# Projecting the selected keys and values of two sequences at once, and pricing TensorE's changes of mode in the planner

## The chip, the cores and the metric

The kernel runs on one NeuronCore of a Trainium2 chip, as one program. TensorE (PE) does the matmuls, VectorE (DVE), ScalarE (ACT) and GpSimd (POOL) the elementwise work, and SyncE (SP) issues all DMAs from one queue. The metric is the device time of one launch in microseconds (us), as the median of several runs; before the change it is 1702.44 us (three runs, 1701.02 to 1708.38).

## The reference

One post-norm decoder layer on x of shape (8, 256, 256) in f32: eight sequences of 256 tokens with 256 features. Three blocks follow each other, each with a residual and a layernorm:

```python
x = _layernorm(x + attn(x))          # three attentions, mixed by a gate
x = _layernorm(x + cross_attn(x, ctx))
x = _layernorm(x + moe_ffn(x))       # 8 experts of 256 -> 1024 -> 256, all evaluated
```

The first block holds three attentions of 16 heads with the same queries: over latent keys (causal), over the 64 selected tokens, and over windowed keys (causal). This change touches the second of them:

```python
scores = (x @ w_imp)[..., 0]
_, idx = jax.lax.top_k(scores, KEEP)             # KEEP = 64, per sequence
sel = jnp.take_along_axis(x, idx[:, :, None], axis=1)
ks = (sel @ w_selk)    # 64 x (16 heads x 96)
vs = (sel @ w_selv)    # 64 x (16 heads x 32)
```

The weights w_selk and w_selv are the same for all sequences.

## The kernel before

All of the work is written as Python generators ("threads") that yield operations, and a planner (`Machine`, L119) puts them in order when the program is built. For each operation it holds a guessed duration, and it keeps the time at which each engine is free, at which each buffer was written and used last, and the state of every pool of buffers. In each step (`run`, L213) it takes from each engine's candidates the one that can start first, or among those that can start within 0.1 us of it the one of lowest rank, and commits the earliest of these. The hardware then executes each engine's list strictly in that order, with semaphores for the dependencies; the guessed times only make the order. DMAs go the same way into the one list of SP: a DMA that waits for its buffer holds up all DMAs planned after it.

A thread's rank starts low for early sequences and grows by `AHEAD` = 4 for each sequence (`each`, L812). Attention work ranks by sequence; the experts (L1378) have rank 99, so they fill what attention leaves free on TensorE. The experts of a sequence can start only when both attention blocks of that sequence are done.

Per sequence s and group g of four heads (NHG = 4 groups): `project` (L827) makes queries, windowed keys and selected keys and turns them (rope); `first` (L958) makes the scores; `weighing` the softmax; `products` (L1048) the weighted values. Matmuls in which the contraction or the output has 32 rows run as groups of four in row or column bands of the array (names `s`, `sx`, `pkn`, `pvl` in row bands, `o`, `ox` in column bands; `mm(..., share=4)`); all others use the whole array. `group` (L288) joins matmuls into one planner operation and adds a fixed `extra` to its guessed time: 0.1 us for scores, 0.3 us for products.

Selection (`selection`, L654) works per sequence: scores to one row, eight rounds of top-8 on DVE, positions by a scan, transposed back with two small matmuls (`ppos`), a one-hot matrix on POOL, and the selected rows of x by matmul (`psel`). The result is copied twice over into `selT` (L688 to L704), so that the value projection (`pvs`, L709) yields the 64 selected values once on partitions 0 to 63 and once on 64 to 127; these are copied into the two diagonal blocks of `vs` (L378), of which there is one, so it is filled when the last products of the sequence before have been issued (L707). The selected keys are projected in `project` for each sequence and group: six matmuls of 128x128 weights with 64 columns (`pks`, L871 to L879). `lead(s)` (L724) returns s, so `two_` is never true.

Each f32 matmul of the program appears as two instructions in the profile.

Buffers that matter here: three tiles each for the expert weights W1 and W2 (`load_w`, L513, 512 KB per half expert, also used for staging the attention weights at the start in `rearrange`, L466), and three each for a sequence's x (`xT` transposed and `xr`, L494), which live from the load until the sequence's experts are done.

Of the kernel before, what the change touches and what calls it, by code (L numbers as in the profile page):

```python
# [17 lines left out]
P = 128  # L18
B, T, C = 8, 256, 256
H = 16  # L20
# [12 lines left out]
NEG = -1e30  # L33
LOWEST = -3.4028234663852886e38
QSCALE = 1.0 / math.sqrt(DH)
AHEAD = 4
ENGINES = {
    mybir.EngineType.PE,
# [17 lines left out]
class Op:  # L56
# [4 lines left out]
    def __init__(self, engine, us, outs, ins, issue, lag=0.0, size=0):  # L61
        self.engine, self.us, self.issue, self.lag, self.size = engine, us, issue, lag, size
        self.writes = [k for x in outs for k in Op.blocks(x)]
        self.reads = [k for x in ins for k in Op.blocks(x)]

    @staticmethod
    def blocks(ap):
# [51 lines left out]
class Machine:  # L119
    def __init__(self):  # L120
        self.free = dict.fromkeys(("PE", "DVE", "ACT", "POOL", "SP"), 0.0)
        self.written, self.used, self.touched = {}, {}, {}
        self.slots, self.tag, self.pending, self.given = {}, {}, {}, {}
        self.transfers = 0.0
        self.reserved = {}
        self.urgent = None
        self.threads = []
# [39 lines left out]

    def start(self, op):
        t = self.free[op.engine]
        for name, b in op.reads:  # L170
            if (name, b) not in self.written:
                return math.inf
            eng, at = self.written[name, b]
            t = max(t, at + (0.0 if eng == op.engine else 0.15))
            if b == PSUM and (name, b) in self.used:
                eng, at = self.used[name, b]
                t = max(t, at + (0.0 if eng == op.engine else 0.1))
        for name, b in op.writes:
            if name in self.pending:
                slots = self.slots[self.pending[name]]  # L180
                if len(slots) <= self.reserved.get(self.pending[name], 0):
                    return math.inf
                t = max(t, min(slots) + 0.1)
            else:
                t = max(t, self.given.get(name, -1.0) + 0.1)
            eng, at = self.used.get((name, b), ("", 0.0))
            t = max(t, at + (0.0 if eng == op.engine else 0.1))
            eng, at = self.written.get((name, b), ("", 0.0))
            if not (op.size and eng == op.engine):
                t = max(t, at + (0.0 if eng == op.engine else 0.15))  # L190
        return t

    def commit(self, op, t):
        for name, _ in op.writes:
            if name in self.pending:
                self.take(name)
        op.issue()
        end = self.free[op.engine] = t + op.us
        if op.size:
            self.transfers = max(self.transfers, end) + op.size / 330e3  # L200
            end = self.transfers + 2.5
        end += op.lag
        for k in op.reads:
            self.used[k] = (op.engine, max(end, self.used.get(k, ("", 0.0))[1]))
            self.touched[k[0]] = max(end, self.touched.get(k[0], 0.0))
        for k in op.writes:
            self.written[k] = (op.engine, end)
            self.touched[k[0]] = max(end, self.touched.get(k[0], 0.0))
# [50 lines left out]
def decoder_layer(ctx: ExitStack, tc: tile.TileContext, a: dict, out: bass.AP):  # L259
# [25 lines left out]
        n = in_.shape[0]  # L285
        return Op("PE", 0.11, [out], [in_], lambda: nc.tensor.transpose(out, in_, ident[:n, :n]), lag=0.17)

    def group(ops, extra=0.0):  # L288
        op = Op("PE", sum(o.us for o in ops) + extra, [], [], lambda: [o.issue() for o in ops], lag=0.17)
        op.writes = list(dict.fromkeys(k for o in ops for k in o.writes))  # L290
        op.reads = list(dict.fromkeys(k for o in ops for k in o.reads))
        return op

    def copied(dst, src):

        return V.tensor_copy(dst, src), A.copy(dst, src)
# [22 lines left out]
    def seen(*key):  # L319
        return lambda: (key if len(key) > 1 else key[0]) in done  # L320
# [145 lines left out]
    def rearrange(g):  # L466

        todo = (
            (wq, a["w_up"][0:QL], QL, 1, lambda o, i: V.tensor_scalar(o, i, QSCALE, None, ALU.mult)),
            (wkw, a["w_wink"], P, 2, A.copy),  # L470
            (wks, a["w_selk"], P, 2, G.tensor_copy),
        )
        staged = []
        yield seen("staged", g - 1) if g else seen("inputs")
        if g:
            yield seen("setup")
        for w, src, rows, k, _ in todo:
            t = three([P, 2, HG * DH], ("w1", "w2")[g % 2], "stage")
            staged.append(t)
            yield dma(t[0:rows, 0:k], src[:, bass.ts(g, HG * DH)].rearrange("(k p) c -> p k c", p=rows))  # L480
        done.add(("staged", g))
        for t, (w, src, rows, k, copy) in zip(staged, todo):
            for i in range(k):
                yield copy(
                    w[0:rows, i, g].rearrange("p i (h r) -> p i h r", h=HG),
                    t[0:rows, i].rearrange("p (h i r) -> p i h r", i=3, r=32),
                )
            m.release(t)
        done.add(("parts", g))
# [2 lines left out]
    xTs, xrs, cTs, w1s, w2s = {}, {}, {}, {}, {}  # L492

    def load_sequence(s):  # L494
        xTs[s] = t = three([P, 2, T], "xT", "xT")
        yield dma(t, kp(a["xT"][:, bass.ts(s, T)]))
        xrs[s] = t = three([P, 2, C], "xr", "xr")
        yield dma(t, a["x"][bass.ts(s, T), :].rearrange("(t p) c -> p t c", p=P))
        done.add(("x", s))

# [12 lines left out]
    def load_w(kept, tag, shape, source):  # L513

        yield seen("parts", NHG - 1)
        for n in range(B * E * 2):
            t = three(shape, tag, tag)
            yield dma(t, source(n // 2 % E, n % 2))
            kept[n] = t

# [133 lines left out]
    def selection(s, d):  # L654
# [36 lines left out]
        else:  # L691
            yield lambda: "selT" in pro[s - 1]
            both = pro[s - 1]["selT"]
        selT = both[:, :, 2 * n : 2 * n + 2]
        pg = mtile([P, 2, KEEP], "psel")
        yield group(
            [
# [3 lines left out]
            ]  # L701
        )
        m.release(hot)
        yield V.tensor_copy(selT, pg.unsqueeze(2).to_broadcast([P, 2, 2, KEEP]))  # L704
        m.release(pg)
        done.add(("selected", s))
        if s:  # L707
            yield seen("products", s - 1, NHG - 1)
        pv = mtile([P, H * VH], "pvs")  # L709
        yield group(  # L710
            [mm(pv, selT[:, k].rearrange("p i s -> p (i s)"), wvs[:, k, :], k == 0, k == 1) for k in range(2)]
        )
        used(lead(s))
        for i in range(2):
            yield copied(vs[bass.ts(i, KEEP), i], pv[bass.ts(i, KEEP)])
        m.release(pv)
        done.add(("selected values", s))

    def used(s):
        pro[s]["users"] -= 1  # L720
# [2 lines left out]

    def lead(s):  # L724

        return s

    def raw(s, d):

# [97 lines left out]
    def project():  # L827
        for s in range(B):
            yield 2 + AHEAD * s
            d = pro.setdefault(s, {})  # L830
            for g in range(NHG):
# [30 lines left out]

                ks = None
                if lead(s) == s:
                    two_ = False
                    yield seen("selected", s)
                    if two_:
                        yield seen("selected", s + 1)
                        stash = kept[g] = four([P, 3, KEEP], "stash", "stash")
                        yield m.claim(stash)  # L870
                    ks = mtile([P, 3, 1 + two_, KEEP], "pks")  # L871
                    sel = d["selT"][:, :, 1 : 3 if two_ else 2].rearrange("p k i s -> p k (i s)")
                    yield group(
                        [
                            mm(ks[:, i].rearrange("p n s -> p (n s)"), wks[:, k, g, i], sel[:, k], k == 0, k == 1)
                            for i in range(3)
                            for k in range(2)
                        ]
                    )  # L879
                    if g == NHG - 1:  # L880
                        used(s)
                    if two_:
                        yield copied(stash, ks[:, :, 1])
                    own = ks[:, :, 0]
                else:
                    own = kept[g]
# [21 lines left out]
    def latent_pairs(name):  # L908

        for s in range(B):  # L910
            yield 2 + AHEAD * s
            d = pro.setdefault(s, {})
            for g in range(2):
# [13 lines left out]
                        ops += [(p_[:, bass.ts(i, P)], lk[rows, bass.ts(i, P)], wkv[rows, g, 1]) for i in range(2)]  # L927
                if name != "kn":
                    ops = ops[0::2] + ops[1::2]
                yield group([mm(*op, share=2) for op in ops], 0.1)  # L930
                for n, p_ in enumerate(ps):
                    yield copied(t[:, n], p_)
                m.release(*ps)
# [6 lines left out]
    def scores(h, d, g, st, which):  # L940
# [4 lines left out]
        for qt, (lo, n) in enumerate(spans):  # L945
            for i in range(3):
                for j in range(HG):
# [5 lines left out]
                    ops.append(  # L953
                        mm(st[j][:, lo : lo + n], h["q"][rows, i, bass.ts(qt, P)], key, i == 0, i == 2, share=4)
                    )
        return group(ops, 0.1)

    def first():  # L958
        for s in range(B):
# [88 lines left out]
    def products():  # L1048
        for s in range(B):
            yield 3 + AHEAD * s  # L1050
            oT = None
            for g in range(NHG):
# [22 lines left out]
                def times(*blocks):  # L1075
                    ops = []
                    for n, (lo, hi, v, src, c) in enumerate(blocks):
                        for j in reversed(range(HG)):
# [7 lines left out]
                                    share=4,  # L1086
                                )
                            )
                    return group(ops, 0.3)

                yield times(
                    (0, T, lambda j: h["vw"][:, 0, bass.ts(j, VH)], pa, 0),
# [39 lines left out]
    def kept_in_dram(shape, name):  # L1132
        d = dram.tile(shape, F32, tag=name, name=name)
        Op.kept.add(d.tensor.name)
        return d
# [67 lines left out]
    def second():  # L1203
        for s in range(B):
# [23 lines left out]
            for g in range(NHG):  # L1228
                pr = three([P, HG * 2 * T], "p", "prx")
                yield m.claim(pr)  # L1230
                if g:
# [6 lines left out]
                        for qt in range(2)  # L1238
                        for j in range(4)
                    ],  # L1240
                    0.1,
                )
                d[g] = {"pr": pr, "st": st}
                done.add(("prx", s, g))
# [32 lines left out]
    def x_products():  # L1277
        for s in range(B):
            yield 3 + AHEAD * s
            for g in range(0, NHG, 2):  # L1280
# [8 lines left out]
                for n in range(2):  # L1289
# [13 lines left out]
                            for c in range(2)  # L1303
                            for j in reversed(range(4))
                        ],
                        0.3,
                    )
                    m.release(xt)
                yield copied(oT[:, g // 2, :], o)
# [143 lines left out]
    each(3, latents)  # L1453
    each(5, selection)
    each(7, gates)
    m.thread(5, context())
    m.thread(5, fetch())
    m.thread(99, experts())
# [96 lines left out]
```

## Time and profile before

| what | value |
|---|---|
| median of three runs | 1702.44 us |
| profiled execution | 1705.71 us, of which the span of instructions 1703.9 us |
| PE busy / weight loads (PEld) busy | 1632.8 us (96%) / 1344.4 us (79%) |
| DVE / ACT / POOL busy | 1178.6 / 573.7 / 601.1 us |
| DMA traffic | 326.82 MB, mean 192 GB/s |
| mean granted TensorE clock | 0.980 |
| expert matmuls `ph` and `py` | 2048 instructions each, 483.2 and 470.9 us |
| `pks` and `pvs` | 384 and 32 instructions, 48.0 and 16.5 us |

The busy time of a group is the union of its instructions' spans; matmuls are pipelined, so one of 256 columns spans some 380 ns while such matmuls start 216 ns apart. What a matmul costs the engine is therefore read from the distance of starts in the timeline, not from its own span. The expert matmuls start at 261.8 us; from 1584 us to the end only the experts of the last sequence are left.

### The profile page before, as it was taken

Reading aid. Unit: us, or ns where it says so; the run is one execution under the profiler, and the core shown is the slowest. Engines: PE = TensorE matmul, PEld = TensorE weight load, DVE = VectorE, ACT = ScalarE, POOL = GpSimd, SP = SyncE. Lnnn points to the kernel's source line nnn. Section 1 sums busy time; section 2 is a strip of 40 time slices with the busy share of each in tenths; the row PEclk is TensorE's granted clock in tenths of the full one; section 3 lists DMA queues with packets and bytes.
Section 4 is the critical chain, followed back from the end, with each engine's and each line's share of the span. In section 5 each row is a group of like instructions: output and inputs, shape, how many; then the busy total and the mean of one; then the engine's idle time right before and its main releaser. Section 6 shows DMA issues by size and latency. Waiting matters only on the chain.

```text
span 1703.9 us, 32142 instructions
## 1 busy us (share of the span) xinstructions
PE 1632.8 (96%) x12196; PEld 1344.4 (79%) x12196; DVE 1178.6 (69%) x2602; ACT 573.7 (34%) x2084; POOL 601.1 (35%) x799
## 2 busy tenths in 40 slices
PE   6999789999999999999999999998999999999998
PEld 4787567887788888887888788886888878888887
DVE  5988777777677856677866786677867777454333
ACT  2554453244324243254324343143422443021000
POOL 3766633444225332263323432343332542021000
PEclk8999898999999999999999999999999999999999
DMA  7212314567926686268563767447592687667452
GB/s 251 81 46 92 135 58 171 176 222 263 319 81 237 211 280 211 84 219 292 199 237 119 268 208 239 175 151 277 193 315 63 231 285 252 199 215 259 130 150 79
DMA packets 183785, 326.82 MB, mean 192 GB/s; under 512 B 12864, under 2 KB 105168, under 8 KB 176464
## 3 DMA queue, kind: packets, MB, share of 16 engines
q1 hardware_dynamic: 183632, 324.78, 56.4%
q8 instruction: 97, 1.59, 0.4%
q14 instruction: 56, 0.46, 0.1%
HBM read 235.60 MB, written 89.14 MB: 191 GB/s over the span
## 4 chain that ended last, share of the span: by engine, by line
PE 79%; issue 8%; DVE 7%; DMA 4%; ACT 1%; POOL 1%; SPq 0%; POOLq 0%; DVEq 0%; ACTq 0%
PE ph L280 22%; PE py L280 22%; PE s L280 8%; PE o L280 4%; PE pk L280 3%; PE pyo L280 3%; PE pks L280 2%; PE pv L280 2%; DMA xpt<-prx 2%; PE sx L280 2%; PE pq L280 2%; PE ox L280 2%; DMA prx<-prx 2%; PE pkm L280 1%; DVE pr L98 1%
## 5 line engine op out<-in xcount | busy, mean ns | idle before, releaser
L280 PE MATMUL ph<-xT,w 128*128 128x256 f32 x2048 | 483.2, 386 | 1.4 <-DVE pl L98 0.6
L280 PE MATMUL py<-w,h 128*128 128x256 f32 x2048 | 470.9, 382 | 0.0
L280 PEld LDWEIGHTS ph<-xT,w 128*128 128x128 f32 x2048 | 387.8, 193 | 68.2 <-issue 10.2
L280 PEld LDWEIGHTS py<-w,h 128*128 128x128 f32 x2048 | 385.3, 191 | 60.0 <-issue 7.9
L98 DVE TENSOR_SCALAR h<-ph,b 128x256 f32<-128x256 f32 x323 | 153.9, 481 | 122.1 <-PE ph L280 119.4
L98 ACT ACTIVATE h<-ph,b 128x256 f32<-128x256 f32 x189 | 89.4, 473 | 323.6 <-PE ph L280 316.6
L98 POOL TENSOR_TENSOR prx<-prx,sumsx 128x512 f32<-128x512 f32 x128 | 129.8, 1045 | 150.9 <-DVE sumsx L98 99.8
L98 DVE SCALAR_TENSOR_TENSOR xr<-py,rw,xr 128x256 f32<-128x256 f32 x128 | 61.0, 478 | 152.5 <-PE py L280 152.2
L98 ACT ACTIVATE prx<-sx,nmx 128x256 f32<-128x256 f32 x256 | 117.1, 486 | 67.9 <-DVE nmx L98 47.8
L98 POOL TENSOR_TENSOR kx<-turn 128x64 f32<-128x64 f32 (+1 forms) x128 | 67.0, 541 | 203.3 <-DVE turn L98 195.6
L98 POOL TENSOR_TENSOR pr<-pr,wpr 128x256 f32<-128x256 f32 (+2 forms) x128 | 129.6, 1043 | 0.0
L98 ACT ACTIVATE pl<-pl,nmpl 128x128 f32<-128x128 f32 (+1 forms) x256 | 113.2, 446 | 13.8 <-DVE nmpl L98 11.8
L98 ACT ACTIVATE pr<-pr,nmpr 128x128 f32<-128x128 f32 (+1 forms) x256 | 113.1, 447 | 0.0
L98 DVE TENSOR_TENSOR pr<-s,causal 128x256 f32<-128x256 f32 x128 | 74.2, 580 | 42.7 <-PE s L280 28.3
L98 POOL TENSOR_TENSOR rstd<-var,nhalf 128x2 f32<-128x2 f32 x24 | 17.2, 718 | 230.4 <-DVE var L98 229.8
L280 PE MATMUL s<-kx,q 32*128 32x320 f32 (+1 forms) x1536 | 95.5, 383 | 2.0 <-ACT prx L98 1.9
L98 POOL TENSOR_TENSOR q<-turn 128x256 f32<-128x256 f32 x64 | 45.6, 729 | 138.4 <-DVE turn L98 136.8
L98 POOL TENSOR_TENSOR pl<-pl,wpl 128x512 f32<-128x512 f32 x64 | 92.5, 1466 | 2.7
L98 DVE TENSOR_REDUCE nmx<-sx 128x2 f32<-128x512 f32 x128 | 79.2, 681 | 11.4 <-PE sx L280 11.4
L280 PEld LDWEIGHTS s<-kx,q 32*128 32x128 f32 x1536 | 70.9, 185 | 19.6 <-issue 7.0
L98 DVE TENSOR_TENSOR pl<-s,causal 128x256 f32<-128x256 f32 x128 | 74.5, 582 | 12.0 <-PE s L280 5.8
L98 DVE TENSOR_REDUCE nmpr<-pr 128x4 f32<-128x256 f32 (+2 forms) x128 | 80.3, 672 | 0.0
(213 smaller groups left out, 2437.0 us busy)
## 6 DMA issues: line engine op xcount, KB each, us to landing
w<-in_W SPq DMA_DIRECT2D x256, 512.0 KB
pr<-pr SPq DMA_DIRECT2D x28, 1024.0 KB
pa<-pr SPq DMA_DIRECT2D x28, 1024.0 KB
prx<-prx SPq DMA_DIRECT2D x28, 1024.0 KB
xpt<-prx SPq DMA_DIRECT2D x28, 1024.0 KB
pl<-pl SPq DMA_DIRECT2D x28, 768.0 KB
pb<-pl SPq DMA_DIRECT2D x28, 768.0 KB
xT<-in_xT SPq DMA_DIRECT2D x8, 256.0 KB
```

The source lines that it names most:

```text
L98: return Op(self.name, us, outs, ins, lambda: getattr(self.engine, kind)(*args, **kw))
L280: lambda: nc.tensor.matmul(out, lhsT, rhs, start=start, stop=stop, skip_group_check=share > 1),
```

## The change

Sequences 2 and 3, 4 and 5, and 6 and 7 form pairs; 0 and 1 stay alone. For a pair, the selected rows of both stand side by side in `selT`. The keys are projected for both at once in the first sequence's `project` (128 columns in place of 64); the second's share is copied to a `stash` tile in SBUF. The values are projected for both at once (64 rows each of one output), copied to SBUF, written to DRAM, and read back into the two blocks of `vs` by two DMAs per sequence, in a thread of its own; the sequences that stay alone go the same way. The planner now knows for each TensorE operation whether it is tiled, and adds 0.3 us to the start of a full one after a tiled one and 0.09 us the other way round; the fixed extras shrink. The pools change: W1 and W2 from three tiles to two each, x from three to four; the staging at the start alternates between the W1 and W2 tiles.

```diff
+LEAVE, ENTER = 0.3, 0.09
...
     def start(self, op):
         t = self.free[op.engine]
+        if op.engine == "PE" and self.tiled != op.tiled:
+            t += LEAVE if self.tiled else ENTER
...
         end = self.free[op.engine] = t + op.us
+        if op.engine == "PE":
+            self.tiled = op.tiled
...
-            t = three([P, 2, HG * DH], ("w1", "w2")[g % 2], "stage")
+            t = two([P, 2, HG * DH], ("w1", "w2")[(g + len(staged)) % 2], "stage")
...
-        xTs[s] = t = three([P, 2, T], "xT", "xT")
+        xTs[s] = t = four([P, 2, T], "xT", "xT")
...
-        xrs[s] = t = three([P, 2, C], "xr", "xr")
+        xrs[s] = t = four([P, 2, C], "xr", "xr")
...
-            t = three(shape, tag, tag)
+            t = two(shape, tag, tag)
...
-        yield V.tensor_copy(selT, pg.unsqueeze(2).to_broadcast([P, 2, 2, KEEP]))
+        yield V.tensor_copy(both[:, :, n], pg)
         m.release(pg)
         done.add(("selected", s))
-        if s:
-            yield seen("products", s - 1, NHG - 1)
+        if lead(s + 1) == s:
+            return
+        rows = (n + 1) * KEEP
         pv = mtile([P, H * VH], "pvs")
         yield group(
-            [mm(pv, selT[:, k].rearrange("p i s -> p (i s)"), wvs[:, k, :], k == 0, k == 1) for k in range(2)]
+            [
+                mm(pv[0:rows], both[:, k, 0 : n + 1].rearrange("p n s -> p (n s)"), wvs[:, k, :], k == 0, k == 1)
+                for k in range(2)
+            ]
         )
         used(lead(s))
-        for i in range(2):
-            yield copied(vs[bass.ts(i, KEEP), i], pv[bass.ts(i, KEEP)])
+        sv = one([P, H * VH], "sv", "sv")
+        yield copied(sv[0:rows], pv[0:rows])
         m.release(pv)
-        done.add(("selected values", s))
+        pro[lead(s)]["sv"] = dv = kept_in_dram([P, H * VH], f"sv{lead(s)}")
+        yield dma(dv[0:rows], sv[0:rows])
+        m.release(sv)
+        done.add(("selected values kept", lead(s)))
+
+    def selected_values():
+        for s in range(B):
+            yield 5 + AHEAD * s
+            yield seen("selected values kept", lead(s))
+            if s:
+                yield seen("products", s - 1, NHG - 1)
+            for i in range(2):
+                yield dma(vs[bass.ts(i, KEEP), i], pro[lead(s)]["sv"][bass.ts(s - lead(s), KEEP)])
+            done.add(("selected values", s))
...
     def lead(s):
 
-        return s
+        return s if s < 2 else s - s % 2
...
                 if lead(s) == s:
-                    two_ = False
+                    two_ = lead(s + 1) == s
...
-                    sel = d["selT"][:, :, 1 : 3 if two_ else 2].rearrange("p k i s -> p k (i s)")
+                    sel = d["selT"][:, :, 0 : 1 + two_].rearrange("p k n s -> p k (n s)")
...
-        return group(ops, 0.1)
+        return group(ops, tiled=True)
...
-                    return group(ops, 0.3)
+                    return group(ops, 0.1, tiled=True)
```

The pairs of latent keys and values keep their extra of 0.1 us, the cross-attention scores lose theirs (0.1 to 0) and the cross-attention products theirs (0.3 to 0); all become tiled.

More of the change, by code (lines that the diff above doesn't have):

```diff
@@ L64, in __init__ @@
         self.reads = [k for x in ins for k in Op.blocks(x)]
+        self.tiled = False
     @staticmethod
@@ L124, in __init__ @@
         self.transfers = 0.0
+        self.tiled = False
         self.reserved = {}
@@ L286, in tr, with group @@
         return Op("PE", 0.11, [out], [in_], lambda: nc.tensor.transpose(out, in_, ident[:n, :n]), lag=0.17)
-    def group(ops, extra=0.0):
+    def group(ops, extra=0.0, tiled=False):
         op = Op("PE", sum(o.us for o in ops) + extra, [], [], lambda: [o.issue() for o in ops], lag=0.17)
+        op.tiled = tiled
         op.writes = list(dict.fromkeys(k for o in ops for k in o.writes))
@@ L693, in selection @@
             both = pro[s - 1]["selT"]
-        selT = both[:, :, 2 * n : 2 * n + 2]
         pg = mtile([P, 2, KEEP], "psel")
@@ L929, in latent_pairs @@
                     ops = ops[0::2] + ops[1::2]
-                yield group([mm(*op, share=2) for op in ops], 0.1)
+                yield group([mm(*op, share=2) for op in ops], 0.1, tiled=True)
                 for n, p_ in enumerate(ps):
@@ L1240, in second @@
                     ],
-                    0.1,
+                    tiled=True,
                 )
@@ L1305, in x_products @@
                         ],
-                        0.3,
+                        tiled=True,
                     )
@@ L1455, in decoder_layer @@
     each(7, gates)
+    m.thread(5, selected_values())
     m.thread(5, context())
```

## The prediction

> **What bounds the kernel now.** I read the page first, then busy time by stage, then TensorE's timeline, then the two queues' waits. The page's engine line and its row of slices:
>
> ```profile
> PE 1632.8 (96%) x12196; PEld 1344.4 (79%) x12196; DVE 1178.6 (69%) x2602; ACT 573.7 (34%) x2084; POOL 601.1 (35%) x799
> ...
> PE   6999789999999999999999999998999999999998
> ```
>
> TensorE is busy all the time after the first tenth. [...] Busy time in three stages (columns: length, then PE, PEld, DVE, ACT, POOL busy with counts, clock, DMA share, GB/s):
>
> ```profile
> 0.00:262.00 262.00, 215.82 (x1983) 172.99 (x1984) 196.25 (x475) 121.33 (x423) 148.22 (x214) 0.92 0.33 108
> 262.00:1584.00 1322.00, 1303.54 (x9699) 1072.42 (x9699) 940.72 (x2038) 451.94 (x1660) 451.51 (x585) 0.99 0.63 215
> 1584.00:1704.00 120.00, 113.47 (x516) 98.95 (x516) 41.62 (x90) 0.47 (x1) 1.33 (x2) 0.97 0.40 120
> ```
>
> The last stage is 512 expert matmuls 216 ns apart, 110.6 us of its 113.5, and there PEld is at 82%. The middle stage has the same 81% (1072.4 of 1322), so PEld near 80% is here what a full stream looks like. [...] Before 262 us there are no experts to fill in, and PE idles 46 us.
>
> **Pairing the keys.** The instructions by form, and the timeline (start, length, what):
>
> ```profile
> L280 PE MATMUL pks<-selT,wks 128*128 128x64 f32 x384 | 48.0, 276 | 0.5 <-DVE selT L98 0.5
> ...
> L280 PE MATMUL pv<-wvw,xT 128*128 128x128 f32 x256 | 37.1, 289 | 0.7 <-DVE pr L98 0.6
> ```
>
> ```profile
> 901.35 1.94 PE L280 MATMUL pvs<-wvs,selT 128*128 128x512 f32 x4
> 903.12 1.89 PE L280 MATMUL py<-w,h 128*128 128x256 f32 x8
> ...
> 934.15 1.45 PE L280 MATMUL pks<-selT,wks 128*128 128x64 f32 x12
> 935.44 1.95 PE L280 MATMUL ph<-xT,w 128*128 128x256 f32 x8
> 937.22 1.05 PE L280 MATMUL pv<-wvw,xT 128*128 128x128 f32 x8
> 938.11 1.03 PE L280 MATMUL ph<-xT,w 128*128 128x256 f32 x4
> 939.07 1.15 PE L280 MATMUL sx<-xk,xq 32*128 32x256 f32 x16
> 940.14 1.07 PE L280 MATMUL ox<-xpt,vx 128*32 128x256 f32 x16
> 941.15 4.58 PE L280 MATMUL ph<-xT,w 128*128 128x256 f32 x20
> 945.57 3.62 PE L280 MATMUL py<-w,h 128*128 128x256 f32 x16
> ```
>
> [...] Twelve `pks` of 64 columns take 934.15 to 935.44, 1.29 us, 107 ns each; eight `pv` of 128 columns take 937.22 to 938.11, 0.89 us, 111 ns each. Both load 128 columns of weights, and that sets the pace. So a paired group costs what a single one did, and three pairs times four groups drop 12 groups: 12 x 1.29 = **15.5 us less** (by the rule: 0). I take the row; it is the same form.
>
> **Pairing the values.** A `pvs` group takes 901.35 to 903.12, 1.77 us, whatever the number of its output rows. Eight become five: 3 x 1.77 = **5.3 us less**. Together 20.8 us of TensorE.
>
> **Mode changes.** Four `ph` before `sx` take 938.11 to 939.07, 0.96 for 4 x 0.216 = 0.86: 0.10 to enter. Twenty `ph` after `ox` take 4.42 for 4.32: 0.10 for the first one after. The last tiled matmul costs another 0.1. From all start times in the trace I count 142 entries into tiled work and as many departures, 0.30 us each for both ends together. The planner's 0.39 is therefore near the truth, where it had 0.1 to 0.3 before. It changes the order only where a second tiled group becomes ready within some 0.3 us of the first one's end. No row shows how often; none gives 0, twenty merges (one in seven) give 20 x 0.3 = 6 us. Five is my guess, nearer the low end since the window is short: **1.5 us less**.
>
> **Two weight tiles in place of three.** SP's waits (total, times, longest):
>
> ```profile
> SPq L271 <- PE ph L280: 465.7, 115, 41.0
> SPq L271 <- PE py L280: 352.1, 117, 12.9
> SPq L271 <- DVE pr L98: 55.5, 23, 8.2
> ```
>
> SP stands at nearly every weight load until TensorE frees a tile: the loads come as soon as they can, and depth is what gives them time. I set each load's issue against the update of its semaphore: issue to landing takes a median of 4.3 us, 7.0 at the ninth decile, 9.7 at most; issue follows the release of the third tile back by 0.03 us, at most 2.6. In an unmixed stretch a W2 tile is free for 8 `py` and 32 `ph` before its next use but one, 40 x 0.216 = 8.6 us; W1 for 16 `ph` and 32 `py`, 10.3. Putting every load at the release of the second tile back, with its own duration and in the present order, leaves the tightest of 252 with 3.1 us in hand: no stall. The low end is 0. The high end is one load in ten that meets the longest landing in the shortest window, 25 x (9.7 - 8.6) = 28 us, if the new order puts parked probabilities ahead of weights. I take **1 us more**, near the measured margin.
>
> **The start.** With four x tiles sequence 3 is loaded at once, and `project` of sequence 2 now waits at `pks` for its selection too. That work moves from about 473 to 498 us into the stretch around 230 to 260 us, just where sequence 0's router is due (first `ph` at 261.8). It brings some 11 us of DVE (eight rounds of 0.9 us, then 1.06, 1.10 and 1.31 us) and a few small TensorE groups; its two loads of x (256 KB each) go through SP near 54 us, among loads of small tables that nobody waits for yet. TensorE's waits show what a selection can do when DVE is later than planned:
>
> ```profile
> PE ppos L286 <- DVE gm L98: 7.3, 1, 7.3
> PE ppos L286 <- DVE kx L98: 6.4, 1, 6.4
> ```
>
> Behind `ppos` everything on TensorE stands, and sequence 0's last transposes with it. One more such wait is 6.4 to 7.3 us; hidden it is 0, and an order that uses the 46 idle us better could gain 3. I take **4 us more**, over half of a wait.
>
> **At nothing, with the cover.** Values now pass through DRAM: 5 writes and 16 reads of 128 KB on SP, 21 x 0.38 = 8 us of its issue time. `vs` is refilled between the last `o` of one sequence and the first of the next; the shortest such stretches are 143 to 179 and 322 to 361 us, and two landings of the nearest row (`xk<-ck`, 64 KB, median 4.3 us, worked out as above) need under 10. Without cover it is up to 10 us per sequence. Such a read waits on SP for the last `o`, with weight loads and parkings behind it; the same kind of wait (SP on PE `o`) now totals 11.1 us in four, the longest 5.0, against the 3.1 us in hand. The 12 stash copies of 192 elements are some 0.4 us each (`vw<-pv`, 256 elements, 0.37 to 0.42) against 11 fewer `vs` copies of 0.58: no net load on ACT and DVE; uncovered, they hold a PSUM tile and cost 5 us. Staging in four tiles instead of six delays the third and fourth head groups' weights by a copy and a load, some 7 us each; they were ready at 29 us and are first used at 51 and 83.
>
> **Sum.** 1705.7 - 15.5 - 5.3 - 1.5 + 1 + 4 = 1688.4 for the profiled execution. That execution lies 3.3 us above the median of the runs, so **1685 us**. [...]
>
> **Rivals.** *The freed time turns into waits at the start* (1697): `ppos` of sequence 3 waits a full 7 us and the router of sequence 0, with it all experts, comes 9 us later, so 16 in place of my 4. For it: PE idles there already and two of three selections stalled. Against: sequence 3's rank is the lowest then, and PE has 46 idle us to absorb it. *Weights come late* (1722): the one mechanism is a release-to-landing beyond the 8.6 us window in stretches of experts. Sequence 7's experts and the mixed middle are 252 loads; 84 of them late by 0.45 us mean 38 us more than the sum. It undoes the gain once lateness totals 18 us. For it: landings up to 9.7 us and a queue in which others stand ahead; against: margins of 3.1 us and more, and in the last stage only weights use the queue. *The order gains more* (1668): twenty merges and 12 of the 18 idle us in the middle gone, since planned and real TensorE time agree better. *The pricing changes no order* is 1686.5, inside the main case.
>
> **How the numbers follow.** Main case 0.70, own range 1674 to 1695; waits at the start 0.15; late weights 0.11; larger gain 0.04. Within 0.5% means 1693.9 to 1711.0, about what a measurement can tell here (three runs lie 0.43% apart). Of the main case 0.05 falls in there, of the waits at the start a third below and 0.02 above it, of the late weights 0.01 in it: faster 0.74, same 0.14, slower 0.12. The range 1670 to 1708 leaves out about 0.05 below and 0.14 above.
>
> **What would show it.** `pks` at 240 instructions and `pvs` at 20, `pks` still near 107 ns apart; PE busy some 21 us lower; the middle stage's idle still below 25 us; first `ph` between 260 and 270 us; no wait of `ph` or `py` on `w<-in_W`. A long wait on those DMAs, or first `ph` after 275 us, makes the prediction wrong; PE busy down by 5 only would mean that paired keys cost double.

## The result, and the profile after

The changed kernel takes 1732.92 us (median, 1723.54 to 1736.36); the kernel before took 1702.75 us beside it (1701.02 to 1708.38). The ratio is 1.0163 with a 95% interval of 1.0138 to 1.0189: **1.6% slower**, where 1685 us was predicted. The profiled execution took 1730.33 us, with a span of 1728.6 us and a mean granted TensorE clock of 0.969 (before: 1705.71, 1703.9 and 0.980).

The page's engine line, its row of forty slices and the clock row of the changed kernel:

```profile
PE 1628.8 (94%) x12040; PEld 1334.1 (77%) x12040; DVE 1196.3 (69%) x2633; ACT 560.8 (32%) x2057; POOL 602.2 (35%) x796
...
PE   6899788999997999999999899999999999999998
PEclk8999988999998999999999899999999999999999
```

TensorE has 156 instructions fewer and 4.0 us less busy time, not 21. The seventh, thirteenth and 23rd slice are no longer full, and the clock digit is 8 in the same three (in the kernel before, in the seventh alone of them). The same three stages as before (length, then PE, PEld, DVE, ACT, POOL busy with counts, clock, DMA share, GB/s):

```profile
0.00:262.00 262.00, 216.85 (x1976) 171.71 (x1976) 197.60 (x483) 117.13 (x405) 143.60 (x205) 0.92 0.33 109
262.00:1584.00 1322.00, 1274.03 (x9427) 1041.32 (x9427) 948.17 (x2041) 441.75 (x1648) 457.20 (x589) 0.98 0.62 213
1584.00:1730.00 146.00, 137.87 (x639) 121.03 (x637) 50.54 (x111) 1.90 (x4) 1.40 (x2) 0.98 0.47 140
```

The start is as before. In the middle stage TensorE now idles 1322 - 1274.0 = 48.0 us, against 18.5 before, and issues 272 matmul instructions fewer there, though the change took away only 156 in all. The last stage has 123 more than before and, with the span, ends 24.7 us later.

**The removed work is really gone.** The selected projections by form, and one pair in TensorE's timeline:

```profile
L287 PE MATMUL pks<-selT,wks 128*128 128x128 f32 x144 | 18.2, 276 | 0.0
L287 PE MATMUL pks<-selT,wks 128*128 128x64 f32 x96 | 13.1, 291 | 0.4 <-DVE selT L100 0.4
L287 PE MATMUL pvs<-wvs,selT 128*128 128x512 f32 x12 | 5.6, 593 | 0.0
L287 PE MATMUL pvs<-wvs,selT 128*64 128x512 f32 x8 | 5.2, 795 | 0.0
```

```profile
738.54 1.50 PE L287 MATMUL pks<-selT,wks 128*128 128x128 f32 x12
739.88 1.88 PE L287 MATMUL pvs<-wvs,selT 128*128 128x512 f32 x4
```

The paired `pks` group of twelve takes 738.54 to 739.88, 1.34 us, where a single one took 1.29. Counted from each matmul's start to the next one's over the whole trace, idle time left out, `pks` went from 43.3 to 28.2 us and `pvs` from 15.4 to 10.5: 20.0 us less.

To see where these went I split TensorE's time, from its first matmul to its last, into three: idle, which is that time less PE's busy time on the page; the half-clock loss, which is half of the busy time in stretches where the granted clock is 0.5; and the rest, matmuls running at the full clock. (In such a stretch, 461.9 to 465.3 us of the kernel before, `ph` matmuls start 0.43 us apart in place of 0.216, so half of that time is lost.)

| us | running | idle | half-clock loss |
|---|---|---|---|
| before | 1607.5 | 59.5 | 25.3 |
| changed | 1591.1 | 87.8 | 37.7 |
| difference | -16.4 | +28.3 | +12.4 |

The sum, +24.3, is the growth of the span (24.7) to within 0.4 us. The work shrank nearly as planned; the waiting grew by more, and some of the work that followed the waits ran at half clock. Between the kernels below whose work is the same, "running" still differs by up to 9 us, so that column is good to several us only. Its mean is 1610.0 us over the six kernels without pairs and 1589.7 over the ten with them: 20.3 us, near the 20.0 counted above.

**What one such wait looks like.** The largest new wait, in TensorE's, DVE's and ACT's timelines of the changed kernel between 549 and 562 us (start, length, what; in brackets the idle time before it and what ended it):

```profile
550.93 1.12 PE L287 MATMUL sx<-xk,xq 32*128 32x256 f32 x13
559.99 1.51 PE L287 MATMUL o<-pa,vw 128*32 128x256 f32 x16 [7.93 <-ACT prx L100]
```

```profile
549.19 0.41 DVE L100 MAX8 m<-left 1x8 f32<-1x256 f32 x1
...
555.99 1.41 DVE L100 TENSOR_TENSOR_SCAN sc<-left 1x256 f32<-1x256 f32 x1
557.44 0.41 DVE L100 TENSOR_TENSOR sc<-sc,left 1x256 f32<-1x256 f32 x1
557.78 2.47 DVE L100 TENSOR_REDUCE nmx<-sx 128x2 f32<-128x512 f32 x4
```

```profile
558.91 0.47 ACT L100 ACTIVATE prx<-sx,nmx 128x256 f32<-128x256 f32 x1 [8.80 <-DVE nmx L100]
```

The scores `sx` are done at about 552 us. Their row maxima `nmx` stand on DVE behind the rest of a later sequence's selection (the last six top-8 rounds from 549.2, scan, positions to 557.8). ACT waits 8.8 us for the maxima, and TensorE 7.9 us for ACT's exponentials: the matmul that would have run needs a PSUM tile, and all eight of the kernel's pool hold scores (four `s`, four `sx`). The experts, which usually fill such a hole, can't get in. The planner's own guess has a hole of 7.4 us at the same place, so no operation came late here: the order itself does this. The same stretch by windows (columns as above):

```profile
548.00:554.50 6.50, 3.93 (x64) 3.11 (x58) 6.16 (x21) 2.11 (x10) 1.85 (x2) 1.00 1.06 398
554.50:565.00 10.50, 5.01 (x58) 3.39 (x59) 10.40 (x19) 3.76 (x16) 2.36 (x3) 0.51 0.42 164
565.00:575.00 10.00, 10.00 (x98) 7.81 (x98) 9.61 (x21) 2.82 (x7) 4.04 (x4) 1.00 0.62 204
```

After the hole the 5.0 us of matmuls up to 565 run at a granted 0.51. The sixteen `o<-pa,vw` among them take 1.28 us (559.99 to 561.27); sixteen of the same forms take 0.68 at a granted 1.00 (458.32 to 459.00). Halved in this way, the 5.0 us would be some 2.5 at full clock, and by this estimate the wait of 7.9 us cost 10.4.

### The profile page after: what moved, and what is told of

The parts are those of the page before. It is cut to its first block, busy times and chain, and to the rows that moved or that the text cites. A ratio compares the mean times of both kernels' runs of the same rounds, so it can differ in the third digit from the quotient of the medians.

```text
span 1728.6 us, 31939 instructions
## 1 busy us (share of the span) xinstructions
PE 1628.8 (94%) x12040; PEld 1334.1 (77%) x12040; DVE 1196.3 (69%) x2633; ACT 560.8 (32%) x2057; POOL 602.2 (35%) x796
## 4 chain that ended last, share of the span: by engine, by line
PE 76%; DVE 9%; DMA 5%; POOL 3%; issue 2%; ACT 1%; POOLq 0%; DVEq 0%; SPq 0%; ACTq 0%
PE py L287 23%; PE ph L287 23%; PE s L287 7%; PE o L287 3%; PE pyo L287 2%; PE pk L287 2%; DMA xpt<-prx 2%; PE ox L287 2%; PE sx L287 2%; DVE pr L100 1%; DVE nmx L100 1%; PE pv L287 1%; DMA prx<-prx 1%; PE pq L287 1%; PE pkm L287 1%
## 5 line engine op out<-in xcount | busy, mean ns | idle before, releaser
L100 DVE TENSOR_SCALAR h<-ph,b 128x256 f32<-128x256 f32 x335 | 159.7, 481 | 146.5 <-PE ph L287 144.4
L100 ACT ACTIVATE h<-ph,b 128x256 f32<-128x256 f32 x177 | 83.9, 475 | 383.1 <-PE ph L287 377.9
L100 DVE TENSOR_TENSOR pr<-s,causal 128x256 f32<-128x256 f32 x128 | 74.5, 582 | 54.4 <-PE s L287 54.4
L287 PE MATMUL s<-kx,q 32*128 32x192 f32 (+1 forms) x1536 | 95.7, 384 | 0.4 <-POOL kx L100 0.3
```

The lines of the kernel that those rows point to most:

```text
L100: return Op(self.name, us, outs, ins, lambda: getattr(self.engine, kind)(*args, **kw))
L287: lambda: nc.tensor.matmul(out, lhsT, rhs, start=start, stop=stop, skip_group_check=share > 1),
```

## The experiments

The changed parts are the pricing (mode changes of TensorE), the pools (two tiles each for W1 and W2, four for x), and the pairs with the values through DRAM. The expectations name these theories. A: pricing moves the order for the worse. B: the pairs make attention work come in bunches. C: weights come late with two tiles. D: the order is a draw; any small change of the guesses moves it as far as this change did, and the holes are in the plan already. E and F: the fourth x tile lets attention run ahead of the experts. The planner's "due time" is its own guess of the end, printed when the order is made; it is no measurement.

All results; the ratio is to the kernel before on the same chip, and idle and half-clock loss are from the split above:

| kernel | median us | ratio (95%) | idle | half-clock loss |
|---|---|---|---|---|
| pairs and pools, no pricing | 1696.2 | 0.9958 (0.9941 to 0.9975) | 68.5 | 19.9 |
| before + pricing | 1704.2 | 1.0009 (0.9990 to 1.0028) | 59.6 | 20.9 |
| before + all new pools | 1717.1 | 1.0078 (1.0061 to 1.0095) | 64.4 | 27.2 |
| before + two weight tiles | 1704.1 | 1.0002 (0.9986 to 1.0017) | 56.8 | 27.7 |
| change without pairs | 1749.9 | 1.0270 (1.0252 to 1.0288) | 90.5 | 32.5 |
| change, LEAVE 0.22 | 1709.8 | 1.0026 (1.0011 to 1.0041) | 77.7 | 32.8 |
| change, LEAVE 0.28 | 1747.1 | 1.0247 (1.0220 to 1.0275) | 101.5 | 38.9 |
| change, LEAVE 0.34 | 1747.9 | 1.0260 (1.0228 to 1.0293) | 103.1 | 41.4 |
| pairs and pools, no pricing, paced | **1676.9** | 0.9849 (0.9824 to 0.9873) | 54.4 | 16.6 |
| the same, tie window 0.12 | 1718.0 | 1.0078 (1.0051 to 1.0104) | 79.2 | 38.4 |
| change (LEAVE 0.30), paced | 1724.5 | 1.0122 (1.0089 to 1.0155) | 83.2 | 36.3 |
| change, LEAVE 0.28, paced | 1703.0 | 1.0003 (0.9989 to 1.0016) | 72.9 | 29.0 |
| change, LEAVE 0.34, paced | 1696.3 | 0.9952 (0.9929 to 0.9975) | 71.4 | 28.7 |
| before, two guesses altered | 1730.9 | 1.0161 (1.0133 to 1.0189) | 72.8 | 31.7 |

**One part at a time.** The pairs and pools without the pricing, and the pricing alone on the kernel before:

```diff
 # pairs and pools, no pricing: the changed kernel with
-LEAVE, ENTER = 0.3, 0.09
+LEAVE, ENTER = 0.0, 0.0
 # and the old extras of 0.1 for scores and 0.3 for products
```

> Pairs and pools of the change, but the planner prices no change of mode and has its old fixed extras. Theory A (the new pricing reorders the work so that TensorE stands in front of PSUM tiles and half-clock windows follow): the 20 us of TensorE from the pairs come through, about 1686 us, 0.8 to 1.2% under before; idle of TensorE near 65 us. Theory B (the pairs themselves starve or bunch the attention, whatever the pricing): about 1720 to 1733 us, idle above 85 us. Theory C (fewer weight tiles): as B.

```diff
 # before + pricing: the kernel before with
+LEAVE, ENTER = 0.3, 0.09
...
+        if op.engine == "PE" and self.tiled != op.tiled:
+            t += LEAVE if self.tiled else ENTER
...
-        return group(ops, 0.1)
+        return group(ops, tiled=True)
 # and so on for the other tiled groups
```

> The kernel before with the pricing of mode changes alone. Theory A: slower than before by the size of the loss, about 1730 to 1755 us. Theory B and theory C: no change beyond 0.5%, 1694 to 1711 us.

Without the pricing the changed kernel takes 1696.2 us, 36.7 less than with it; the pricing alone, on the old kernel, does nothing (1704.2). The first is neither theory A's 1686 nor theory B's 1720 and more; the second is 26 us under the least that theory A allowed. Then the pools alone, and the change with the pairs undone:

```diff
 # before + all new pools: the kernel before with
-            t = three([P, 2, HG * DH], ("w1", "w2")[g % 2], "stage")
+            t = two([P, 2, HG * DH], ("w1", "w2")[(g + len(staged)) % 2], "stage")
...
-        xTs[s] = t = three([P, 2, T], "xT", "xT")
+        xTs[s] = t = four([P, 2, T], "xT", "xT")
...
-        xrs[s] = t = three([P, 2, C], "xr", "xr")
+        xrs[s] = t = four([P, 2, C], "xr", "xr")
...
-            t = three(shape, tag, tag)
+            t = two(shape, tag, tag)
```

> The kernel before with two weight tiles each, four x tiles and the new staging, no pairs and no pricing. Theory C (weights arrive late): slower, 1720 us or more, with waits of expert matmuls on weight loads. Theories A and B: within 0.5% of before, 1694 to 1711 us.

```diff
 # change without pairs: the changed kernel with
-        return s if s < 2 else s - s % 2
+        return s
```

> The changed kernel with every sequence alone (pricing, pools and values through DRAM stay). Theory A: slower than the change by the 20 us of TensorE that the pairs save, about 1753 us. Theory B: back near before, 1695 to 1712 us.

The pools alone cost 13 to 14 us (1717.1). Pairs on top of them, both without pricing, bring 1717.1 - 1696.2 = 20.9; with pricing they bring 1749.9 - 1732.9 = 17.0. Both are near the 20.8 of the prediction, though with orders that differ as much as shown below, such closeness of single differences is partly luck. Undoing the pairs does not lower TensorE's idle time (90.5 us against 87.8), so theory B falls. What is left is odd: pricing costs 0 on the old kernel and 36.7 on the new one, and about as much on the new pools without pairs (1749.9 - 1717.1 = 32.8, where the values' way through DRAM differs as well). Either it collides with the new pools, or the order is a draw.

**Is the price itself at fault?** The same kernel with other prices, and the weight tiles alone:

```diff
 # the changed kernel with 0.22, 0.28 or 0.34
-LEAVE, ENTER = 0.3, 0.09
+LEAVE, ENTER = 0.22, 0.09
```

> The changed kernel with LEAVE 0.22 in place of 0.3. Theory D (the order is a lottery: a small change of the constant moves it as much as the whole change did, and each order carries its stalls in the planner's own due times, which the chip follows): the planner's last due time falls from 1721.7 for 0.3 to 1700.0, so about 1707 us, 22 us under the change. Theory A (pricing near the true cost is what makes the stalls): within 8 us of the change, 1725 to 1741.

> The changed kernel with LEAVE 0.28. Theory D: the planner's last due time rises to 1744.1, so about 1752 us, 20 us over the change. Theory A: within 8 us of the change, 1725 to 1741.

> The changed kernel with LEAVE 0.34. Theory D: the planner's last due time is 1752.4, so about 1760 us. Theory A: 1730 to 1745, a little above the change since the constant is larger.

```diff
 # before + two weight tiles: as the new pools above, but x stays at three
-            t = three(shape, tag, tag)
+            t = two(shape, tag, tag)
```

> The kernel before with two tiles each for W1 and W2 (and the staging that fits them), three x tiles. Theory C (weights late): 1715 us or more, with the loss of the new pools. Theory E (the loss of the new pools comes from the fourth x tile, which lets attention run ahead of the experts): within 0.5% of before, 1695 to 1712 us, with no wait of expert matmuls on a weight load.

0.22, 0.28, 0.30 and 0.34 give 1710, 1747, 1733 and 1748 us. A price that is wrong by so much cannot do that: between 0.28 and 0.30 lie 0.02 us for each of some 140 departures, 2.8 us, and the time falls by 14, and 0.34 is back at 1748. What remains is that the number decides which of nearly equal candidates comes first; the planner's due times move with it (1700.0, 1744.1, 1721.7 and 1752.4). The two weight tiles cost nothing (1.0002), and neither `ph` nor `py` waits for a weight there or in the changed kernel: theory C falls. Of the new pools' 13 us, then, the fourth x tile is what is left, or the draw of the order.

**The fourth x tile.** A view of one tile, the router's logits `plg`, whose last start is when the last sequence's attention is done; kernel before with all new pools first, then with two weight tiles only (minimum, median, maximum in ns, then first and last start in us):

```profile
L280 PE MATMUL plg<-wr,xT x64: 172/256/380, 241.1 to 1480.1; 128*128 128x8 f32 x64
```

```profile
L280 PE MATMUL plg<-wr,xT x64: 172/256/379, 261.5 to 1578.2; 128*128 128x8 f32 x64
```

With a fourth x tile attention ends 98 us sooner, and nothing is won by it: 1715.4 - 1480.1 = 235 us of expert work stand behind it instead of 1704.6 - 1578.2 = 126. Experts fill TensorE's holes while attention waits; those that are left for the end fill none. The middle stages of the same two kernels:

```profile
262.00:1584.00 1322.00, 1293.49 (x9637) 1059.02 (x9634) 933.47 (x1997) 449.42 (x1662) 452.27 (x588) 0.99 0.62 212
```

```profile
262.00:1584.00 1322.00, 1305.81 (x9707) 1074.63 (x9708) 940.64 (x2039) 452.18 (x1660) 453.66 (x587) 0.99 0.62 215
```

PE is busy 12.3 us less in the first. The same view of the kernel before, the changed kernel, and pairs and pools without pricing:

```profile
L280 PE MATMUL plg<-wr,xT x64: 172/256/379, 260.1 to 1579.2; 128*128 128x8 f32 x64
```

```profile
L287 PE MATMUL plg<-wr,xT x64: 173/256/379, 262.7 to 1550.8; 128*128 128x8 f32 x64
```

```profile
L287 PE MATMUL plg<-wr,xT x64: 173/256/277, 247.4 to 1515.3; 128*128 128x8 f32 x64
```

In the changed kernel 178 us follow the last `plg`, in place of 125 before. But without the pricing it is also 1693.0 - 1515.3 = 178 us, and that kernel is 36.7 us faster: the long end is not what sets these two apart. Idle time and half clock are: 87.8 + 37.7 us against 68.5 + 19.9, 37 us in all. The middle stage without the pricing idles 1322 - 1288.6 = 33.4 us in place of 48.0:

```profile
262.00:1584.00 1322.00, 1288.57 (x9582) 1059.11 (x9582) 943.23 (x2029) 450.63 (x1663) 451.08 (x585) 0.99 0.63 216
```

With three x tiles no sequence could begin before the experts of the one three ahead of it had given a tile back; the third tile was a pace-maker as well as a buffer. If that is a cause, giving the pace back while keeping the tile must help:

```diff
 # paced: at the start of project(s)
+            if s >= 3:
+                yield seen("experted", s - 3)
 # and at the end of experts(s)
+            done.add(("experted", s))
```

> Pairs and pools without pricing, and the projection of sequence s waits in the planner until the experts of s - 3 have been issued, as three x tiles enforced before (all other work as in the run with pairs and no pricing). Theory F (the fourth x tile lets odd sequences' attention run ahead of the experts, and that costs the gain): the planner's last due time falls from 1698.3 to 1678.0, so about 1676 us, 1.6% under before. Theory D alone (a lottery of orders, pace has no part): no preference, 1690 to 1725 us.

> The changed kernel with LEAVE 0.28, which took 1747 us, with the same pace. Theory F: the planner's last due time falls from 1744.1 to 1709.8, so about 1712 us. Theory D alone: a new draw, 1700 to 1750 us with no direction.

> The changed kernel as it is, with the same pace. Here the planner's last due time does not move (1721.7 to 1721.9), so theory D expects 1724 to 1735 us, no change; theory F as a rule without exceptions expects 1710 us or less.

> The changed kernel with LEAVE 0.34, which took 1748 us, paced. Theory D with F: the planner's last due time falls from 1752.4 to 1699.7, so about 1698 us. Theory A (pricing near the true cost makes the stalls, whatever the draw): no better than the paced change at 0.3, 1715 us or more.

Four kernels, each with and without the pace: 1696.2 to **1676.9** (no pricing), 1747.1 to 1703.0 (0.28), 1732.9 to 1724.5 (0.30), 1747.9 to 1696.3 (0.34). Three are clearly faster, by 19 to 52 us. The change itself gains 8 us, within the spread of the runs (1723.5 to 1736.4 without the pace, 1718.7 to 1727.1 with it). There the planner's due time did not move either (1721.7 to 1721.9), and theory F without exceptions had asked for 1710 or less. So the missing pace is not shown to be what the change itself lost by. The first of the four beats both kernels; its page and its middle stage:

```profile
PE 1609.4 (96%) x12040; PEld 1320.8 (79%) x12040; DVE 1162.2 (69%) x2584; ACT 576.9 (34%) x2105; POOL 602.4 (36%) x797
...
PE   6899789999999999999999999999999999999998
```

```profile
262.00:1584.00 1322.00, 1302.82 (x9662) 1070.11 (x9662) 936.83 (x2025) 454.74 (x1678) 452.63 (x585) 1.00 0.64 218
```

PE busy is 23.4 us below the kernel before, the middle stage idles 19.2 us, and the last `plg` starts at 1536.0, 140 us before the end. The gain is larger than the prediction's sum, and not all of it is the pairs: by the split 14.7 us are running, 8.7 half-clock loss and 5.1 idle time. `py` waits once for a weight, 0.9 us.

**How much is a draw.** Two kernels keep the work and the pools of their twins; only the planner's guesses or its tie window are nudged:

```diff
 # before, two guesses altered
-        us = 2 * 0.00084 * max(free_size(rhs), free_size(lhsT)) / share
+        us = 2 * 0.000845 * max(free_size(rhs), free_size(lhsT)) / share
...
-    ... .get(kind, 0.15 + 0.00106 * n)
+    ... .get(kind, 0.152 + 0.00106 * n)
```

> The kernel before, same work and same pools, with two guesses of the planner moved: 0.845 in place of 0.84 ns per column and pass of a matmul, 0.152 in place of 0.150 us fixed per VectorE operation. Theory D (any kernel of this planner is one draw): the planner's last due time rises from 1703.3 to 1726.6, so about 1725 us. If only the change's kernels are sensitive: within 0.5% of before, 1695 to 1712 us.

```diff
 # pairs and pools, no pricing, paced, with a tie window of 0.12
-... if x[0] <= first + 0.1 ...
+... if x[0] <= first + 0.12 ...
```

> The paced pairs without pricing (1676.9 us), with the planner's window for taking the lower rank at 0.12 in place of 0.1 us. Theory D: the planner's last due time rises from 1678.0 to 1704.5, so about 1703 us: part of the 1676.9 was a good draw. If pairs and pace alone make the gain: 1672 to 1684 us.

The kernel before, with two of the planner's guesses moved by about 1%, takes 1730.9 us, as slow as the changed kernel. Its page and its `plg`:

```profile
PE 1643.6 (95%) x12196; PEld 1348.5 (78%) x12196; DVE 1189.1 (69%) x2619; ACT 568.7 (33%) x2070; POOL 599.9 (35%) x796
```

```profile
L280 PE MATMUL plg<-wr,xT x64: 172/256/277, 284.1 to 1588.8; 128*128 128x8 f32 x64
```

It has all 12,196 matmul instructions of the kernel before, but its first `plg` comes at 284.1 us, 24 later than before (260.1), so that TensorE has no experts to fill in for that much longer, and the last one comes 10 later. And the paced kernel with another tie window takes 1718.0, 41 us more than its twin and more than either expectation. So theory D stands: one draw of the order is worth about as much as the whole change, and 1676.9 is partly a good draw.

**The planner's own end.** Theory D's expectations are made from the planner's due times, and these tell the outcome well. For the twelve kernels whose due time is on record, from 1678.0 to 1752.4, the measured median lies between 7 us below it and 14 us above it. The change had 1721.7 there and the kernel before 1703.3. The planner itself, before any run, put the change 18 us behind; the prediction did not use that number.

**What is settled and what is not.** Shown: the pairs save what was worked out; with two weight tiles an expert matmul waits for a weight at most once in a kernel, 1.0 us at the longest; the loss is TensorE's idle time with the half clock behind it, and the order carries it, for a nudge of two guesses makes the kernel before as slow with all its work unchanged. Shown too, for this one pair of kernels: without the pricing the change is 36.7 us faster. Not shown is why. The pricing was neutral on the old kernel; on the new pools without the pace all five priced kernels (1710 to 1750) are slower than their unpriced twins (1696 and 1717); with the pace an unpriced draw (1718) is slower than two of three priced ones (1696, 1703, 1724). It may do harm of its own with these pools (theory A in a narrower form), or be one more nudge of the order (theory D). Supported by four clear comparisons of one sign (the pools alone against two weight tiles alone, and three paced kernels), and by a fifth within the noise: the fourth x tile without a pace is worse. With draws this wide, its size is not settled. The mechanism (bunched attention, PSUM full of scores) was seen at one place; for the other holes it is argued.

## Why the prediction was wrong

By its own steps:

- *Pairing the keys, 15.5 us less*: right, 15.1, and not the 0 that stands beside it. A group with 128 columns costs 1.34 us where one with 64 costs 1.29. In both the twelve weight loads keep PEld busy for 1.50 of 1.52 us (from 738.33 us with 128 columns, from 933.94 us of the kernel before with 64).
- *Pairing the values, 5.3 us less*: right, 4.9. At the full clock a group took 1.83 us with 64 output rows (at 95.6 us) and 1.72 to 1.81 with 128.
- *Mode changes, 1.5 us less for five merges*: entries fell from 142 to 137 and departures too; the five were called a guess, and as a number they came out. **But this is the step that failed.** It let the price change the order "only where a second tiled group becomes ready within some 0.3 us of the first one's end", and asked only how many changes of mode that saves. With everything else of the change in place, the price cost 36.7 us (1732.9 against 1696.2) where 1.5 were to be gained. It did so through the order: the middle stage idles 48.0 us with it and 33.4 without it. What in the price does this stays open.
- *Two weight tiles, 1 us more*: measured at nothing (1.0002), and no expert matmul of the changed kernel waits for a weight.
- *The start, 4 us more*: the first `ph` comes at 264.5 instead of 261.8, 2.7 later, near the 4. The wait named did not make it. The changed kernel's waits of `ppos`:

```profile
PE ppos L293 <- DVE sc L100: 8.1, 2, 5.2
...
PE ppos L293 <- DVE gm L100: 6.9, 1, 6.9
```

  The 6.9 us are sequence 0's, at 26.6 us, as before (7.3). Sequence 2's wait of 6.4 us at 195.1 is gone. Sequence 3's is the one of 5.2, but it comes at 286.1 us, after the first `ph`. In all `ppos` waits 15.0 us in place of 13.7, and TensorE's idle time before 262 us is 45.1 us in place of 46.2.

- *At nothing*: the values through DRAM made no wait of TensorE's that shows. SP did stand for them, 25.0 us in five waits for `sv`, and this part was not tried by itself. But the fourth x tile is in the sum only as two early loads and one early selection. A pool's size was read as memory and not as what kept attention within three sequences of the experts. The pools alone cost 13 to 14 us on the old kernel; in the change itself the pace brought 8 us back, within the noise.

Behind both stands a premise that no step stated: that the order of before would hold, so that savings subtract from it one by one. "The middle stage's idle still below 25 us" was the test of that, and it came out at 48.0. "PE busy down by 5 only would mean that paired keys cost double" came true in its number (4.0) but not in its reading: of the 16.4 us that running lost, 12.4 came back as matmuls at half clock, which count as busy for twice as long (`ph` 0.43 us apart in place of 0.216). One reading of the rows was off without weight for the sum: TensorE is not "busy all the time after the first tenth", for the fifth and sixth slices of the row shown there (170 to 256 us) have 7 and 8 tenths.

Of the rivals, the waits at the start (1697) showed up in small; late weights (1722) gave about the right size by a mechanism that does not occur; the larger gain by a better order (1668) came true nowhere, and the nearest, the paced 1676.9, has no pricing, which was to be its cause. None had the order itself turning worse, as it did when two guesses were nudged. Slower had a chance of 0.12, but all of it for late weights and waits at the start, not for what happened. The result lies 25 us above the range of 1670 to 1708, about the width of one draw.

## What to carry to other kernels

When a greedy planner makes the order, work that is taken away is a gain only if the new order keeps the engine fed: read the planner's own end first (1721.7 against 1703.3 here), then the idle time of the fed stage, and set the width of the forecast by how far the same kernel moves when a guess of the planner is nudged by a per cent (here about 27 us of 1703). Before a pool grows, ask what its scarcity was pacing, and try an explicit condition in its place. Judge an edit by several draws with and without it, and then ship the best draw: pairs and pools with the pace and without the pricing, at 1676.9 us, 1.5% below the kernel before.

## What the runs showed of the hardware

Idle time of TensorE was not all that was lost here. In the windows shown above the granted clock is 1.00 up to 554.5 us, 0.51 from there to 565 us, around and after a hole of 7.9 us, and 1.00 again behind that. Over the whole kernel, idle time rose by 28.3 us and the half-clock loss by 12.4, together 1.4 us for each added idle microsecond. That is no fixed price: pairs and pools without pricing idle 9.0 us more than the kernel before and lose 5.4 us less to the half clock. In the long hole the last matmul ends at 552.05 us, and from 554.5 us, 2.5 us later, the clock is down. In the kernel before, it is down from 461.9 us, behind two shorter waits close together, 1.88 us before 460.3 us and 0.45 before 461.2. TensorE's windows there:

```profile
458.00:461.90 3.90, 1.57 (x8) 0.79 (x7) 2.81 (x16) 0.58 (x2) 0.70 (x1) 1.00 0.97 325
461.90:465.30 3.40, 3.40 (x9) 2.28 (x8) 1.42 (x4) 0.47 (x1) 0.00 (x0) 0.50 1.06 382
465.30:470.00 4.70, 4.70 (x24) 4.13 (x22) 2.42 (x5) 0.00 (x0) 0.00 (x0) 1.00 0.46 142
```

Between 461.9 and 465.3 us the clock is 0.50, for 3.4 us, with TensorE busy throughout. The prediction had priced each wait at its own length.
